# Tying five chunks' router logits to the shared expert's progress, and adding three chunks' shared results later, in a fused spike and mixture-of-experts kernel

## The chip, the cores and the metric

The kernel runs on one core of a Trainium2 chip. The core has five engines that this document names often: TensorE (PE in the profile; its weight loads are shown apart as PEld), VectorE (DVE), ScalarE (ACT), GpSimd (POOL) and SyncE (SP), whose queue issues most transfers. The metric is the device time of one launch in microseconds; less is better.

## The reference, cut to what matters

The input `x` is 16 sequences of 256 rows with 256 columns in f32, together 4096 rows. A first layer adds spikes to it, and a second adds a mixture of experts with one shared expert:

```python
rates = relu(x) * 0.001
c = cond[:, None, :] + cumsum(rates, axis=1)
spikes = floor(c) - previous_floor(c)          # along the 256 rows
x = x + spikes / 0.001

shared = silu(xf @ w1) * (xf @ w3) @ w2        # 256 -> 512 -> 256
s = sigmoid(concat([xf, cond], -1) @ router_W) # 8 experts
_, topk_idx = top_k(s + router_bias, 2)
gates = s_sel / (sum(s_sel) + 1e-9)
h = gelu(xf @ W1e[e]);  y = h @ W2e[e]         # the two experts of a row, 256 -> 256 -> 256
x = x + (shared + gates[0] * y[0] + gates[1] * y[1]) / 3
```

## The kernel before, in words

The 4096 rows are cut into 8 chunks of 512 (`NCHUNK`, `N`). A chunk i passes these steps.

- `Spikes` and `elementwise(i)` (from L264 and L491). TensorE turns the chunk so that columns lie on partitions (L294), ScalarE writes rates and a copy (L301, L310), VectorE forms the running sums (L323, L332, L337), ScalarE adds the starting state and rounds (L347, L356), and VectorE takes the floor, the differences and the sum `x1` (L369, L370, L381, L389).
- `route(i)` (L522) is a generator of eight steps, taken with `next(ro)`. First the logits: 8 products of `x1` with the router's weights on TensorE (L535), then `lt` on VectorE (L544), a turn `pn` on TensorE (L547), an exponential on ScalarE (L551), some twenty small VectorE instructions that pick the two experts (L553 to L590), the places in the experts' lists on TensorE (`pr`, L596 to L602), `x1` turned back by TensorE (L618) and copied to `x1t` by ScalarE (L619), the rows' addresses `at_i` on VectorE (L632), and eight indirect stores of `x1t` into the buffer `xs` in DRAM, issued by POOL (L636), some 1.28 us apart.
- The shared expert, `shared_hidden(i)` and `shared_out(i)`. A hidden step is, for each of four column blocks u, two pairs of products (L659, into `ph`), a silu on ScalarE (L669) and a multiplication on VectorE (L670, into `hs`). An output step is 16 products (L686, into `pa`, two halves of 512 columns), and for each half a VectorE instruction that multiplies by a third and adds to `x1t` (L697). All products are f32, and a product is two instructions in the profile.

The shared expert has no deadline until the end, and the kernel uses it to fill TensorE. `all_shared()` (L717) yields its steps in the order hidden 0, hidden 1, out 0, hidden 2, out 1 and so on, and `unit(n)` (L728) takes n units from it wherever the program calls it. One unit is 4 hidden products or 8 output products. With `whole` left true, a unit that ends a pair also emits the ScalarE and VectorE instructions behind it.

The program has five stages. A head (L744 to L806) handles chunk 0 and begins chunk 1. A loop (L829) runs route(i-1), elementwise(i) and (i+1) and units. In the tail (from L853) the last chunk's route runs, then the experts' counts (`pcnt`, L866), a table of 128-row blocks on VectorE (L873 to L917), two small products (L920, L924), and between these the units `unit(0.5)` (L858), `unit(2, whole=False)` (L862), `unit(2.5)` (L918) and `unit(3)` (L927). Then come the expert blocks (`run_blocks`): six blocks are loaded ahead by transfers on SP's queue and on ScalarE's (L956), `unit(1)` fills TensorE once more, and then for each block VectorE copies the weights (L971, `load_w`) and turns the rows (L976), TensorE multiplies (L1003, `up`), ScalarE applies gelu (L1011), TensorE multiplies (L1025, `down`), ScalarE copies (L1033) and POOL stores the result (L1034). A last stage gathers the results, combines them with the gates (L1141) and runs what is left of the shared expert.

In the head and in the tail with the blocks, the order on TensorE, ScalarE and VectorE is the order of the program (`manual_schedule`). In the loop a planner decides when the program is built: each engine takes, of what is ready by the planner's own clock, what stands earliest in the program. It may take instructions of the loop into gaps of the head. At run time every engine executes its list in order and waits on semaphores.

Outputs leave when both the shared and the routed part of a row tile are done (`part_done`, L707), which is in the last stage for all chunks.

Of the kernel before, what the change touches and what calls it, by code (L numbers as in the profile page):

```python
# [38 lines left out]
def kernel(  # L39
# [83 lines left out]

    busy = const.tile([P, N], BF16)
    nc.vector.memset(busy, 0.0)
# [136 lines left out]
    class Spikes:  # L262
# [256 lines left out]

    placed = {}  # L520

    def route(i):  # L522
        x1, x1t = x1s[i], x1ts[i]

        def small(tag, shape=(P, J, E), dt=F32):
            return rt.tile(list(shape), dt, tag=tag, name=f"{tag}_{i}")

# [5 lines left out]
        for k in range(KD):  # L533
            for j in range(J):
                nc.tensor.matmul(  # L535
                    pl[ts(j, 32), :],
                    lhsT=rw[:, k, :],
                    rhs=x1[:, k, ts(j, P)],
                    start=(k == 0),
                    stop=(k == KD - 1),  # L540
                )
        yield
        lt = small("lt", (P, P))
# [99 lines left out]

    hts = {}

    def shared_hidden(i, slices):
# [3 lines left out]
        for cols in slices:  # L652
            n = cols.stop - cols.start
            for u in range(KS):
                ps = []
                for w in (w1_sb, w3_sb):
                    ph = p_h.tile([P, n], F32, tag="ph", name=f"ph_{i}_{u}_{cols.start}_{len(ps)}")
                    for k in range(KD):
                        nc.tensor.matmul(  # L659
                            ph,  # L660
                            lhsT=w[:, k, ts(u, P)],
                            rhs=x1[:, k, cols],
                            start=(k == 0),
                            stop=(k == KD - 1),
                        )
                    ps.append(ph)
                    yield n / N / 2, len(ps) == 2
# [9 lines left out]
    def shared_out(i):  # L677
# [4 lines left out]
        for h in range(J // n):  # L682
            pa = p_acc.tile([P, n, D], F32, tag="acc", name=f"pa_{i}_{h}")
            for q in range(n):
                for s in range(KS):
                    nc.tensor.matmul(  # L686
                        pa[:, q, :],
# [13 lines left out]
            yield 0, False  # L701


# [125 lines left out]
    for i in range(2, NCHUNK):  # L829
# [14 lines left out]
        next(nxt, None)  # L844
        unit(1 + (i > 3 and i % 3 != 2) + (i == NCHUNK - 1))
        next(ro)
# [64 lines left out]

    diag = const.tile([P, P], BF16)
# [3 lines left out]
    rows_f = const.tile([P, NBLK], F32)  # L916
# [9 lines left out]
    nc.vector.tensor_copy(rows_i[:, :NBLK], prow)  # L926
    unit(3)  # L927

# [271 lines left out]
```

## Time and profile before

| what | us |
|---|---|
| median of 10 runs | 332.92 (332.72 to 333.17) |
| the profiled execution | 332.96 |
| its span in the profile | 331.2 |
| busy: PE, PEld, DVE, ACT, POOL | 322.8, 236.9, 224.5, 142.4, 160.4 |
| last logits (L535) start | 129.54 |
| first expert block (L1003) starts | 163.37 |
| last stage's products (L659) start | 283.07 |

The span is the time from the first to the last instruction. A line of the timeline gives start, duration, engine, source line, operation, output and inputs, how many instructions were merged, and in brackets how long the engine was idle ahead and what ended that. "PEld ... issue" is time in which nothing that the profile shows was waited for. An engine name with a q is its queue issuing transfers. The granted TensorE clock was full in every slice.

### The profile page before, as it was taken

To read this page: it belongs to the slowest core of one execution; us is meant where nothing else is said; L and a number is where in the kernel's file an instruction comes from. 1 tells how busy PE (TensorE), PEld (TensorE's weight loads), DVE (VectorE), ACT (ScalarE), POOL (GpSimd) and SP (SyncE) were. 2 spreads that over 40 slices of the span, in tenths; PEclk is the share of its full clock that TensorE was granted. 3 is DMA by queue.
4 is the path that set the end of the run, shared out by engine and by line. 5 is a ranking of instruction groups with operands and counts; after the bars stand their busy time and mean duration, and the time that the engine had idled before them with its cause. 6 is when DMAs were issued, how large, how long until landed. Compare 5 with 4: busy or idle time off the path is not lost. (4 is left out here: it accounts for less than half of the span.)

```text
span 331.2 us, 6640 instructions
## 1 busy us (share of the span) xinstructions
PE 322.8 (97%) x1734; PEld 236.9 (72%) x1734; DVE 224.5 (68%) x612; ACT 142.4 (43%) x301; POOL 160.4 (48%) x199
## 2 busy tenths in 40 slices
PE   8999999999999999999999999999999999999996
PEld 3877554546646645746699999999999999465485
DVE  5786879889999994642467654554555552089993
ACT  4449294948568363040244444444444444301100
POOL 6000671787877777172045555555555555223220
PEclk9999999999999999999999999999999999999999
DMA  7561827474212122054446667766666752499933
GB/s 235 165 145 48 225 100 189 152 213 154 95 54 98 66 83 102 30 194 108 75 101 146 149 156 161 149 153 129 153 148 144 169 144 83 135 376 410 405 113 127
DMA packets 62550, 50.36 MB, mean 152 GB/s; under 512 B 42622, under 2 KB 52879, under 8 KB 62512
## 3 DMA queue, kind: packets, MB, share of 16 engines
q1 hardware_dynamic: 42928, 26.21, 31.6%
q0 software_dynamic: 7456, 20.86, 17.2%
q10 hardware_dynamic: 12128, 2.86, 5.1%
q8 instruction: 15, 0.25, 0.3%
q14 instruction: 23, 0.19, 0.2%
HBM read 27.44 MB, written 22.84 MB: 152 GB/s over the span
## 5 line engine op out<-in xcount | busy, mean ns | idle before, releaser
L659 PE MATMUL ph<-x,w_sb 128*128 128x512 f32 (+2 forms) x320 | 118.8, 513 | 1.6 <-DVE x L487 0.7
L1034 POOL DMA_INDIRECT ys<-yb,to x67 | 65.9, 984 | 67.1 <-ACT yb L1033 57.3
L636 POOL DMA_INDIRECT xs<-x1t,at_i x64 | 74.3, 1162 | 42.0 <-issue 16.8
L659 PEld LDWEIGHTS ph<-x,w_sb 128*128 128x128 f32 x320 | 53.6, 190 | 44.0 <-issue 38.1
L1003 PEld LDWEIGHTS phe<-xbt,w1e 128*128 128x128 f32 x536 | 70.3, 191 | 4.7 <-ACT hbt L1011 0.9
L1003 PE MATMUL phe<-xbt,w1e 128*128 128x128 f32 x536 | 70.7, 275 | 0.7 <-DVE xbt L976 0.7
L1025 PE MATMUL py<-we,hbt 128*128 x268 | 68.8, 380 | 0.0
L686 PE MATMUL pa<-w_sb,hs 128*128 128x256 f32 x256 | 59.7, 383 | 0.0
L971 DVE COPY w1e<-we 128x512 f32 x67 | 28.8, 431 | 44.8 <-PE phe L1003 44.3
L686 PEld LDWEIGHTS pa<-w_sb,hs 128*128 128x128 f32 x256 | 47.4, 190 | 9.5 <-issue 3.8
L669 ACT ACTIVATE as<-ph 128x512 f32<-128x512 f32 (+2 forms) x40 | 20.5, 516 | 68.1 <-PE ph L659 65.0
L1025 PEld LDWEIGHTS py<-we,hbt 128*128 128x128 f32 x268 | 45.9, 191 | 3.6
L1011 ACT ACTIVATE hbt<-phe 128x256 f32<-128x256 f32 x67 | 25.7, 383 | 44.7 <-PE phe L1003 36.3
L670 DVE TENSOR_TENSOR hs<-as,ph 128x512 f32<-128x512 f32 (+2 forms) x40 | 23.0, 575 | 29.8 <-PE ph L659 23.4
L1033 ACT COPY yb<-py 128x256 f32<-128x256 f32 x67 | 24.9, 372 | 23.1 <-PE py L1025 23.0
L976 DVE STREAM_TRANSPOSE xbt<-xb 128x256 f32<-128x256 f32 x67 | 29.3, 437 | 0.2
L323 DVE TENSOR_TENSOR_SCAN tb<-keep,rates 128x1024 f32<-128x1024 f32 (+1 forms) x9 | 17.3, 1925 | 0.0
L712 POOL DMA_DIRECT2D out_dram<-yc x8 | 5.8, 727 | 22.7 <-DVE yc L1141 22.7
L573 POOL COPY x1t<-first 128x16 f32<-128x16 f32 x8 | 4.4, 548 | 24.5 <-DVE first L571 24.5
L347 ACT ACTIVATE tb<-tb,cond_t 128x256 f32<-128x256 f32 x30 | 13.1, 498 | 6.4 <-DVE tb L337 6.4
L697 DVE SCALAR_TENSOR_TENSOR x1t<-pa,x1t 128x512 f32<-128x512 f32 x14 | 9.6, 684 | 7.7 <-PE pa L686 7.7
L619 ACT COPY x1t<-px 128x512 f32<-128x512 f32 x16 | 8.9, 585 | 7.7 <-PE px L618 7.7
(152 smaller groups left out, 278.7 us busy)
## 6 DMA issues: line engine op xcount, KB each, us to landing
xb<-xs SPq DMA_DIRECT2D x184, 33.0 KB
yc<-ys SPq DMA_DIRECT2D x8, 512.0 KB
we<-ys SPq DMA_DIRECT2D x8, 512.0 KB
xn<-in_x_dram SPq DMA_DIRECT2D x7, 512.0 KB
xb<-xs ACTq DMA_DIRECT2D x84, 33.0 KB
we<-in_L_cond_W1e_dram SPq DMA_DIRECT2D x8, 256.0 KB
we<-in_L_cond_W2e_dram SPq DMA_DIRECT2D x8, 256.0 KB
out_dram<-yc POOLq DMA_DIRECT2D x8, 256.0 KB, 5.5
```

The source lines that it names most:

```text
L636: nc.gpsimd.indirect_dma_start(out=xs_w[(i * J + j) * TOPK + q][:, :], out_offset=bass.IndirectOffsetOnAxis(ap=at_i[:, q, j : j + 1], axis=0),
L659: nc.tensor.matmul(ph, lhsT=w[:, k, ts(u, P)], rhs=x1[:, k, cols], start=(k == 0), stop=(k == KD - 1),)
L669: nc.scalar.activation(act, ps[0], AF.Silu)
L670: nc.vector.tensor_tensor(ht[:, u, cols], act, ps[1], ALU.mult)
L686: nc.tensor.matmul(pa[:, q, :], lhsT=ht[:, s, ts(n * h + q, P)], rhs=w2_sb[:, s, :], start=(s == 0), stop=(s == KS - 1),)
L971: nc.vector.tensor_copy(w, we[:, bass.ds(off, KD * HE)])
L976: nc.vector.transpose(xt.rearrange("p g k r -> p g (k r)"), block[b].pop("xb")[:, :, :FQ])
L1003: nc.tensor.matmul(ph[:, m, :].rearrange("p (g r) -> p g r", r=Q), lhsT=w[:, k, ts(m, P)], rhs=xt[:, :, k, :], start=(k == 0), stop=(k == ...
L1011: nc.scalar.activation(ht, ph, AF.Gelu)
L1025: nc.tensor.matmul(py, lhsT=ht[:, k, :], rhs=we[:, bass.ds(off + KD * HE + k * D, D)], start=(k == 0), stop=(k == KH - 1),)
L1033: nc.scalar.copy(yb, py)
L1034: nc.gpsimd.indirect_dma_start(out=ys_w[b][:, :], out_offset=bass.IndirectOffsetOnAxis(ap=to[:, b : b + 1], axis=0), in_=yb, in_offset=Non ...
```

## The change

A counter `made` collects the shared expert's products in program order. `STEP` names, for chunks 2 to 6, a number of products; the logits of that chunk get an ordering edge (no wait at run time) that lets the planner place them on TensorE only after that product. In the loop, each i from 3 on takes half a unit more; the tail takes 1.5 units in place of 2.5, and three half units in place of 3. The results of chunks 0, 1 and 2 (`LATER`) are no longer added to `x1t` by VectorE out of the accumulator: ScalarE writes them, times a third, over the chunk's `x1`, which nobody reads any more, and VectorE adds them (`add_third`) in the tail, two after each half unit. So that `x1` stays that long it has 8 buffers in place of 6, `first` and `at_i` have 8 in place of 2, and three small tiles move into buffers of other tiles. The condition that held back chunk 0's addition until chunk 1 was placed is gone.

```diff
-    busy = const.tile([P, N], BF16)
+    busy = hid.tile([P, N], BF16, tag="ht", name="busy")
...
-                [P, KD, N], F32, tag="x1", name=f"x1_{self.i}", bufs=6
+                [P, KD, N], F32, tag="x1", name=f"x1_{self.i}", bufs=8
...
+    logits = {i: [] for i in range(NCHUNK)}
+    STEP = {2: 84, 3: 100, 4: 120, 5: 140, 6: 156}
+    made = []
+
+    def in_step(i):
+        if i in STEP and logits[i] and len(made) >= STEP[i]:
+            for m in logits[i]:
+                tc.add_manual_dep(
+                    m.ins,
+                    made[STEP[i] - 1].ins.name,
+                    mybir.DependencyInfo(
+                        mybir.DependencyClass.NoSync, mybir.DependencyReason.DATA
+                    ),
+                    reason="order on TensorE",
+                )
+
+    def shared_matmul(*args, **kwargs):
+        made.append(nc.tensor.matmul(*args, **kwargs))
+        for i, n in STEP.items():
+            if n == len(made):
+                in_step(i)
...
-        key_first = small("first", (P, J))
+        key_first = small("first", (P, J), bufs=NCHUNK)
...
-        at_i = small("at_i", (P, TOPK, J), I32)
+        at_i = small("at_i", (P, TOPK, J), I32, bufs=NCHUNK)
...
+    LATER = 3
+    thirds = []
...
-            with tc.issue_after(placed[1].ins) if i == 0 else nullcontext():
-                nc.vector.scalar_tensor_tensor(
-                    bs, pa.rearrange("p q (g f) -> p q g f", f=FQ), THIRD, bs, ALU.mult, ALU.add
-                )
+            if i < LATER:
+
+                third = x1s[i].rearrange("p k n -> p (k n)")[:, ts(h, n * D)]
+                nc.scalar.activation(third, pa.rearrange("p q d -> p (q d)"), AF.Copy, scale=THIRD)
+                thirds.append((i, h * n, bs, third))
+                yield 0, False
+                continue
+            nc.vector.scalar_tensor_tensor(
+                bs, pa.rearrange("p q (g f) -> p q g f", f=FQ), THIRD, bs, ALU.mult, ALU.add
+            )
             part_done(i, h * n, n)
             yield 0, False
+
+    def add_third():
+
+        i, j, bs, third = thirds.pop(0)
+        nc.vector.tensor_tensor(
+            bs, bs, third.rearrange("p (q g f) -> p q g f", q=wide(i), f=FQ), ALU.add
+        )
+        part_done(i, j, wide(i))
...
-        unit(1 + (i > 3 and i % 3 != 2) + (i == NCHUNK - 1))
+        unit(1 + (i > 2) / 2 + (i > 3 and i % 3 != 2) + (i == NCHUNK - 1))
...
-    unit(2.5)
+    unit(1.5)
...
-    unit(3)
+    for _ in range(LATER):
+        unit(0.5)
+        add_third()
+        add_third()
```

In `shared_hidden` and `shared_out` the products are made by `shared_matmul`, and the logits of `route` are kept in the list `logits[i]`, followed by a call of `in_step(i)`. The tiles `diag` and `rows_f` of the tail take buffers of the tile `lt`.

More of the change, by code (lines that the diff above doesn't have):

```diff
@@ L1 @@
 import itertools
-from contextlib import ExitStack, nullcontext
+from contextlib import ExitStack
 import numpy as np
@@ L520, with small @@
     placed = {}
+    logits = {i: [] for i in range(NCHUNK)}
[17 more added lines that the diff above has]
+                in_step(i)
     def route(i):
         x1, x1t = x1s[i], x1ts[i]
-        def small(tag, shape=(P, J, E), dt=F32):
-            return rt.tile(list(shape), dt, tag=tag, name=f"{tag}_{i}")
+        def small(tag, shape=(P, J, E), dt=F32, **kw):
+            return rt.tile(list(shape), dt, tag=tag, name=f"{tag}_{i}", **kw)
         def wide(a):
@@ L534, in route @@
             for j in range(J):
[L535 to L540, printed above, removed]
+                logits[i].append(
+                    nc.tensor.matmul(
+                        pl[ts(j, 32), :],
+                        lhsT=rw[:, k, :],
+                        rhs=x1[:, k, ts(j, P)],
+                        start=(k == 0),
+                        stop=(k == KD - 1),
+                    )
                 )
+        in_step(i)
         yield
@@ L658, in shared_hidden @@
                     for k in range(KD):
-                        nc.tensor.matmul(
+                        shared_matmul(
                             ph,
@@ L685, in shared_out @@
                 for s in range(KS):
-                    nc.tensor.matmul(
+                    shared_matmul(
                         pa[:, q, :],
@@ L694, in shared_out @@
             bs = final.get((i, h * n), x1ts[i][:, ts(h, n), :, :FQ])
[L696 to L699 removed]
+            if i < LATER:
[7 more added lines that the diff above has]
+            )
             part_done(i, h * n, n)
             yield 0, False
+    def add_third():
+        i, j, bs, third = thirds.pop(0)
+        nc.vector.tensor_tensor(
+            bs, bs, third.rearrange("p (q g f) -> p q g f", q=wide(i), f=FQ), ALU.add
+        )
+        part_done(i, j, wide(i))
     done = {t: 0 for t in range(NTT)}
@@ L910 @@
     nc.vector.tensor_copy(table, table_f)
-    diag = const.tile([P, P], BF16)
+    diag = rt.tile([P, P], BF16, tag="lt", name="diag")
     nc.vector.tensor_scalar(which, which, -1.0, float(E), ALU.mult, ALU.add)
     nc.vector.tensor_scalar(diag, ident, which, None, ALU.mult)
-    rows_f = const.tile([P, NBLK], F32)
+    rows_f = rt.tile([P, NBLK], F32, tag="lt", name="rows_f")
     nc.vector.tensor_scalar(rows_f, ident[:, :NBLK], table_f[:, 0:1], None, ALU.mult)
-    unit(2.5)
+    unit(1.5)
     pcode = p_t.tile([P, NBLK], F32, tag="pt", name="pcode")
```

## The prediction

> **What bounds the kernel now.** I read the page's busy shares first, then the busy time by stretch, then TensorE's waits and its instructions in order of time, and last the other engines around the hand-over to the expert blocks.
>
> ```profile
> PE 322.8 (97%) x1734; PEld 236.9 (72%) x1734; DVE 224.5 (68%) x612; ACT 142.4 (43%) x301; POOL 160.4 (48%) x199
> ...
> 36.40:129.50 93.10, 91.66 (x427) 50.16 (x426) 83.02 (x190) 58.89 (x102) 66.40 (x59) 1.00 0.42 127
> 129.50:163.40 33.90, 33.90 (x142) 21.75 (x142) 13.81 (x51) 6.05 (x11) 10.91 (x12) 1.00 0.37 103
> 163.40:282.10 118.70, 117.96 (x805) 110.71 (x803) 66.44 (x216) 51.20 (x134) 63.97 (x65) 1.00 0.62 141
> ...
> PE pr L597 <- DVE hot L590: 1.1, 3, 0.6
> PE pn L547 <- DVE lt L544: 0.2, 1, 0.2
> ```
>
> After the clock interval each window line gives busy time of PE, PEld, DVE, ACT and POOL. TensorE is busy all the time, but its ends are modelled, so I look at the distance between starts. In the combine stage, where the chain that ended last is TensorE alone, 24 hidden instructions take from 283.07 to 293.47, 0.43 us each, and 32 output ones 0.216 us. In the middle stretch the same spacings hold: 22 hidden instructions between 119.92 and 129.54 are again 0.43 apart. Subtracting such spacings from the starts between 36.4 and 129.5 leaves only 2.7 us in which TensorE stood for another engine (0.72 at 53.2, 0.39, 0.53 and 0.25 ahead of L597, 0.37 ahead of L547, some 0.4 in smaller ones; the two wait lines are the part that outlasts the modelled ends). VectorE is 89% busy there, but TensorE reaches the last chunk's logits 3.6 us after their input was ready: the last L389 ends at 125.94, L535 starts at 129.54.
>
> The next two fences are the hand-over in order of time: TensorE, then POOL, SP's queue, VectorE and ScalarE.
>
> ```profile
> 119.92 9.69 PE L659 MATMUL ph<-x,w_sb 128*128 128x512 f32 x22
> 129.54 0.64 PE L535 MATMUL pl<-x,rw 128*32 128x128 f32 x16
> 130.12 1.99 PE L686 MATMUL pa<-w_sb,hs 128*128 128x256 f32 x8
> 131.95 0.27 PE L547 MATMUL pn<-ident,lt 128*128 128x128 f32 x1
> ...
> 139.05 0.40 PE L596 MATMUL pr<-region,ones_r 1*128 1x32 f32 x2
> ...
> 140.43 0.17 PE L866 MATMUL pcnt<-counts_b,ones_b 128*128 128x8 bf16 x1
> ...
> 159.94 3.60 PE L659 MATMUL ph<-x,w_sb 128*128 128x512 f32 x8
> 163.37 1.05 PE L1003 MATMUL phe<-xbt,w1e 128*128 128x128 f32 x8
> 165.16 1.13 PE L1003 MATMUL phe<-xbt,w1e 128*128 128x128 f32 x8 [0.74 <-DVE xbt L976]
> 166.22 1.10 PE L1025 MATMUL py<-we,hbt 128*128 x4
> ```
>
> ```profile
> 150.49 0.97 POOL L636 DMA_INDIRECT xs<-x1t,at_i  x1 [0.30 <-issue]
> ...
> 152.94 15.76 SPq L956 DMA_DIRECT2D xb<-xs  x26
> ...
> 163.64 0.69 DVE L670 TENSOR_TENSOR hs<-as,ph 128x512 f32<-128x512 f32 x1 [1.63 <-PE ph L659]
> ...
> 153.09 5.51 ACTq L956 DMA_DIRECT2D xb<-xs  x7
> 161.85 0.60 ACT L669 ACTIVATE as<-ph 128x512 f32<-128x512 f32 x1 [9.74 <-PE ph L659]
> ...
> 163.22 1.28 ACT L1011 ACT_TABLE_LOAD   x1 [0.77 <-issue]
> 164.51 0.38 ACT L1011 ACTIVATE hbt<-phe 128x256 f32<-128x256 f32 x1
> ```
>
> This is a second path beside TensorE: logits, route, eight scatters on POOL, their landing, the block loads. The loads start at 152.94, the moment the last scatter has landed; by the landing marks in the trace block 0 is complete at 156.4, block 1 at 158.4, block 3 at 161.5. TensorE comes to block 0 only at 163.37, since the written order puts 6.5 units of the shared expert (1 unit is 8 hidden or 16 output instructions, 3.44 us either way) between pcnt and it. So the path of the data has some slack, and the change spends it.
>
> **The change part by part.** The sum is made against the profiled execution, 332.96 us (span 331.2 and 1.76 around it); the median of the runs is 332.92, no difference.
>
> *Units moved.* The loop gets half a unit more in each of i = 3 to 7; the tail gives back one at the 2.5 and one and a half at the 3. Adding up the units, 160 products stand before the last logits now (a product is two instructions) and 178 then: 16 output products of chunk 3, 32 x 0.216 = 6.91, and 2 hidden ones of chunk 5, 4 x 0.43 = 1.72. TensorE's total is unchanged, but the last logits, and with them the whole second path, come 8.63 us later, less what the middle can absorb. Behind them wait lt, the route on VectorE, POOL's eight scatters, SP's and ScalarE's block loads.
>
> *What the middle absorbs.* The ties put logits of chunks 2 to 6 behind 84, 100, 120, 140 and 156 products; counted in the timeline they stand behind 76, 90, 107, 122 and 140. TensorE then has more to do between two routes and VectorE less, so the 2.7 us of waits can shrink; a whole x1 also keeps the logits in one piece, where now three of five are cut in two (0.92 against 0.57 to 0.75 us), up to 0.7. Bounds 0 and 3.4 us; I take the middle, 1.7, because L597's waits are a chain (lt, exp, twenty small ones) that the ties don't shorten.
>
> *Three chunks' results on ScalarE.* Six L697 leave VectorE's middle, 6 x 0.68; six scaled copies of 128x512 out of PSUM come to ScalarE, bounded by L619 (0.585) and L669 (0.60): 3.6 us on an engine busy 58.9 of 93.1. Nothing in the middle waits for them but the two accumulation buffers, which chunk 0 holds until 56 now. Without that cover the price were 3.6. Since TensorE is the later engine, VectorE's saving is worth nothing by itself; what it could bring is inside the 1.7. No DMA moves: these chunks' outputs leave only in the combine stage.
>
> *Six adds in the tail*, L381 as the nearest row (0.683): 4.1 us on a VectorE busy 13.81 of 33.9, done before block 0 lands. Two or three fall beside the last scatters. Those take 0.97 to 1.50 beside L381 and L389, 0.97 alone: 0 to 0.5, I take 0.2.
>
> *lt behind a product.* Now the unit after the last logits is an output product; lt runs at 130.32 beside it and pn follows at 131.95, 2.41 after the logits began. Then it is the second half of a hidden pair: logits 0.58, four instructions 1.72, 0.18 to the start of L670, 0.6 until lt can start, 0.34, 0.05: pn at 3.47. That adds 1.06 on the second path (0.6 to 1.2 by how early L670 starts). If the planner leaves that pair whole, it is 0.
>
> *The cover at the blocks.* After pcnt TensorE has 4 units instead of 6.5: 14.3 us with the two small products, so on the old clock it stands before block 0 at 154.8, where the data is complete at 156.4. Then the order written out bites: ScalarE issues seven block loads until 158.6 before it may take the hidden activation (L669), VectorE's L670 waits for that (159.3), and load_w(1) and block 1's turn stand behind L670. Today L670 starts at 163.64 and block 1 at 165.16; so block 1 at 160.8. ScalarE's next two loads reuse marks that land at 160.6, then a table load of 1.28 and gelu 0.38: down(0) at about 162.7, today 166.22. The second path gains 3.5 us against TensorE's order, not 8.63. Bounds: 4.3, if gelu is in time, and 3.2, if the loads land 0.3 later. From there the distance of the blocks is 1.75 us as now, all else hidden under TensorE.
>
> *The rest* (the tiles busy, diag and rows_f in other buffers, x1, first and at_i with more) costs no instruction. VectorE's waits in the middle are for ScalarE and TensorE only, never for these buffers, so nothing is gained. POOL: chunk 6's scatters end some 22 us after its logits, chunk 7's begin about 27 after them.
>
> Sum: 8.63 - 1.7 + 0.2 + 1.06 - 3.5 = +4.7, 337.6 us. Its ends: 8.63 - 3.4 + 0 + 0.6 - 4.3 = +1.5 (334.5), and 8.63 - 0 + 0.5 + 1.2 - 3.2 = +7.1 (340.1).
>
> [...]
>
> **The rivals.** *The last logits overtake* (other side): the planner may run them when x1 is ready, ahead of free products. The place is TensorE's order at product 178; each output product overtaken takes 0.43 us off the second path. From 11 on it wins; if all 18 are overtaken the path starts as now, less the 1.7: 331.3 us. For it: their input is ready early. Against: now too they waited 3.6 us for 160 of 160.
>
> *The cover is not needed.* If ScalarE's loads don't hold up L669 and the blocks start as soon as TensorE is there, only the 1.7 and today's wait of 0.9 go: 330.4. Against: block 0 lands 1.6 us after TensorE is ready.
>
> *ScalarE becomes late*: its copies stand before exp or a silu, buffers come free late, some 0.5 us per route for six routes on top of the sum: 340.6. For it: VectorE already waits 0.6 to 1.6 us for L551. Against: 63% load.
>
> *It doesn't do what it says*: the planner finds no place for 18 more products before the last logits and leaves them behind, so neither the path nor the cover moves: 333. Against: its buffers come free earlier than now.
>
> **How the numbers follow.** The sum's case 0.65; milder forms of it, without the lt wait or with pairs overtaken, 333.6 to 334.5, 0.10; overtaking 0.08; cover not needed 0.06; no change 0.05; ScalarE late 0.06. Less than 0.2%, 0.7 us, can't be told from no change. Faster 0.14, same 0.05, slower 0.81. The likeliest case alone spans 334.5 to 340.1; the range with a fair part of the others is 332.6 to 340.2.
>
> **What would show it.** Right: the last L535 about 6 to 8 us later, at 135.5 to 138; L547 stalled about 1 us behind lt; a gap on TensorE before the first L1003 and a second before block 1 with VectorE's xbt as releaser, some 5 us together; L1025 starting near 170.5; the blocks and the combine stage as long as now. Wrong: L535 with fewer than 178 products before it, no gap at the blocks, or waits in the middle that were larger than the 2.7 us I count.

## The result and the profile after

The changed kernel takes 345.66 us (median of 8 runs, 344.60 to 346.37) against 333.04 us of the kernel before (28 runs, 332.72 to 333.77) on the same chips: a ratio of 1.0376, interval 1.0367 to 1.0386. It is 12.6 us slower; the forecast was 4.7 us slower, with 340.2 as its upper end. The profiled execution took 345.54 us (span 343.8), 12.58 above that of before.

The page's busy times and granted clock come first.

```profile
PE 324.6 (94%) x1734; PEld 238.9 (69%) x1734; DVE 225.5 (66%) x612; ACT 146.2 (43%) x307; POOL 159.2 (46%) x199
...
PEclk9999999999999999999959999999999999999999
```

TensorE's busy time has hardly moved (322.8 before), so the loss is idle time; and one slice of the clock reads 5, which no slice of before did. Next the busy time by stretch (after each clock interval PE, PEld, DVE, ACT, POOL, then the clock), cut at the last logits, at block 0, shortly before the return of the clock, and ahead of the combine stage; and TensorE's waits up to the last logits.

```profile
36.40:139.90 103.50, 99.23 (x466) 56.85 (x466) 82.31 (x187) 61.41 (x106) 63.09 (x58) 1.00 0.38 112
139.90:169.10 29.20, 25.55 (x106) 14.59 (x105) 15.52 (x54) 6.13 (x9) 13.03 (x14) 1.00 0.34 110
169.10:180.00 10.90, 6.37 (x27) 5.55 (x28) 4.16 (x13) 2.91 (x5) 0.41 (x1) 0.57 0.44 75
180.00:295.00 115.00, 114.96 (x779) 107.73 (x778) 62.36 (x203) 49.06 (x130) 63.81 (x66) 1.00 0.63 143
```

```profile
PE pr L623 <- DVE hot L616: 2.6, 4, 0.8
PE pn L573 <- DVE lt L570: 1.2, 2, 1.0
```

Line numbers have shifted: L559 is the logits, L573 `pn`, L570 `lt`, L616 `hot`, L623 `pr`, L540 every product of the shared expert, L697 its silu, L698 its multiplication, L739 the late adds, L1000 the block loads, L1020 a block's turn, L1047 and L1069 its two pairs of products, L1055 its gelu. Before the last logits TensorE waits more than before (1.1 and 0.2 us on these two lines then). Behind them it has 3.65 idle us where it had none, then 4.53 in the eleven around the first blocks. The next fence is the hand-over to the blocks, first on TensorE, then on POOL, ScalarE with its queue (ACTq) and VectorE.

```profile
139.88 0.65 PE L559 MATMUL pl<-x,rw 128*32 128x128 f32 x16
...
143.64 0.30 PE L573 MATMUL pn<-ident,lt 128*128 128x128 f32 x1 [1.21 <-DVE lt L570]
...
152.13 0.17 PE L907 MATMUL pcnt<-counts_b,ones_b 128*128 128x8 bf16 x1
...
163.05 3.60 PE L540 MATMUL ph<-x,w_sb 128*128 128x512 f32 x8
169.09 1.16 PE L1047 MATMUL phe<-xbt,w1e 128*128 128x128 f32 x8 [2.45 <-DVE xbt L1020]
174.46 2.04 PE L1047 MATMUL phe<-xbt,w1e 128*128 128x128 f32 x8 [4.21 <-DVE xbt L1020]
176.83 2.07 PE L1069 MATMUL py<-we,hbt 128*128 x4 [0.33 <-ACT hbt L1055]
...
162.24 1.50 POOL L662 DMA_INDIRECT xs<-x1t,at_i  x1 [0.30 <-issue]
...
165.22 6.98 ACTq L1000 DMA_DIRECT2D xb<-xs  x7
172.30 0.60 ACT L697 ACTIVATE as<-ph 128x512 f32<-128x512 f32 x1 [17.55 <-DMA xb<-xs]
172.82 2.25 ACTq L1000 DMA_DIRECT2D xb<-xs  x2
175.10 1.28 ACT L1055 ACT_TABLE_LOAD   x1 [2.19 <-DMA xb<-xs]
...
176.39 0.66 ACT L1055 ACTIVATE hbt<-phe 128x256 f32<-128x256 f32 x2
...
168.59 0.45 DVE L1020 STREAM_TRANSPOSE xbt<-xb 128x256 f32<-128x256 f32 x1 [3.11 <-DMA xb<-xs]
172.93 0.69 DVE L698 TENSOR_TENSOR hs<-as,ph 128x512 f32<-128x512 f32 x1 [3.90 <-ACT as L697]
...
173.88 0.44 DVE L1020 STREAM_TRANSPOSE xbt<-xb 128x256 f32<-128x256 f32 x1
```

It is the picture forecast, only larger: a gap before each of the first two blocks with the turn as releaser, ScalarE's seven load issues ahead of the silu, the silu ahead of VectorE's multiplication, that ahead of block 1's turn. One thing is new: block 1's products last 2.04 us here, where a block's products last 1.05 before. The clock was at half. Two stretches of one us show when (columns as above):

```profile
170.00:171.00 1.00, 0.25 (x3) 0.06 (x1) 0.00 (x0) 0.00 (x0) 0.00 (x0) 0.82 0.43 79
...
180.00:181.00 1.00, 1.00 (x5) 0.91 (x5) 0.35 (x2) 0.35 (x1) 0.59 (x1) 0.56 0.62 95
```

The stretch before the first reads 1.00 and those between the two 0.50, so the clock fell at about 170.65 and came back at about 180.9. At 170.65 the second gap had lasted only 0.4 us: the fall came behind the first gap of 2.45 us and the beginning of the second, with 3.8 of the second's 4.21 us still ahead.

Following the path event by event gives the account. The columns are start times in two profiled executions, and the third is what the step between adds.

| event | before | after | step adds |
|---|---|---|---|
| last logits | 129.54 | 139.88 | +10.34 |
| `pn` of that chunk | 131.95 | 143.64 | +1.35 |
| `pcnt` | 140.43 | 152.13 | +0.01 |
| first block load | 152.94 | 165.22 | +0.58 |
| block 0's second products | 166.22 | 176.83 | -1.67 |
| block 10's first products | 181.21 | 193.81 | +1.99 |
| combine stage | 283.07 | 295.67 | 0.00 |

They add up to 12.60. The 10.34 holds the 8.63 us of moved products, so the middle did not absorb but lost 1.71.

### The profile page after: what moved, and what is told of

The parts are those of the page before. It is cut to its first block, busy times and chain, and to the rows that moved or that the text cites. A ratio compares the mean times of both kernels' runs of the same rounds, so it can differ in the third digit from the quotient of the medians.

```text
span 343.8 us, 6630 instructions
## 1 busy us (share of the span) xinstructions
PE 324.6 (94%) x1734; PEld 238.9 (69%) x1734; DVE 225.5 (66%) x612; ACT 146.2 (43%) x307; POOL 159.2 (46%) x199
## 5 line engine op out<-in xcount | busy, mean ns | idle before, releaser
L540 PE MATMUL ph<-x,w_sb 128*128 128x512 f32 (+2 forms) x320 | 118.7, 513 | 2.5 <-DVE x L487 1.2
L662 POOL DMA_INDIRECT xs<-x1t,at_i x64 | 72.0, 1125 | 53.5 <-issue 16.1
L540 PEld LDWEIGHTS ph<-x,w_sb 128*128 128x128 f32 x320 | 53.9, 190 | 46.6 <-issue 38.8
L1047 PEld LDWEIGHTS phe<-xbt,w1e 128*128 128x128 f32 x536 | 71.9, 196 | 11.1 <-issue 4.4
L1047 PE MATMUL phe<-xbt,w1e 128*128 128x128 f32 x536 | 72.6, 280 | 6.7 <-DVE xbt L1020 6.7
L1069 PE MATMUL py<-we,hbt 128*128 x268 | 70.1, 385 | 0.3 <-ACT hbt L1055 0.3
L540 PE MATMUL pa<-w_sb,hs 128*128 128x256 f32 x256 | 59.4, 382 | 0.0
L540 PEld LDWEIGHTS pa<-w_sb,hs 128*128 128x128 f32 x256 | 47.5, 190 | 9.0 <-issue 3.2
L1069 PEld LDWEIGHTS py<-we,hbt 128*128 128x128 f32 x268 | 46.6, 194 | 4.3 <-ACT hbt L1055 0.6
L697 ACT ACTIVATE as<-ph 128x512 f32<-128x512 f32 (+2 forms) x40 | 20.6, 514 | 66.9 <-PE ph L540 49.1
L1055 ACT ACTIVATE hbt<-phe 128x256 f32<-128x256 f32 x67 | 25.6, 384 | 44.0 <-PE phe L1047 34.7
L698 DVE TENSOR_TENSOR hs<-as,ph 128x512 f32<-128x512 f32 (+2 forms) x40 | 23.0, 577 | 31.1 <-PE ph L540 20.3
L1020 DVE STREAM_TRANSPOSE xbt<-xb 128x256 f32<-128x256 f32 x67 | 29.3, 437 | 3.6 <-DMA xb<-xs 3.6
L599 POOL COPY x1t<-first 128x16 f32<-128x16 f32 x8 | 5.5, 690 | 26.4 <-DVE first L597 26.4
L369 DVE TENSOR_TENSOR tb<-tc,tb 128x1024 f32<-128x1024 int32 (+1 forms) x8 | 9.3, 1156 | 6.4 <-ACT tc L356 6.4
```

What stands on the lines that cost most here:

```text
L540: made.append(nc.tensor.matmul(*args, **kwargs))
L662: nc.gpsimd.indirect_dma_start(out=xs_w[(i * J + j) * TOPK + q][:, :], out_offset=bass.IndirectOffsetOnAxis(ap=at_i[:, q, j : j + 1], axis=0),
L697: nc.scalar.activation(act, ps[0], AF.Silu)
L698: nc.vector.tensor_tensor(ht[:, u, cols], act, ps[1], ALU.mult)
L1020: nc.vector.transpose(xt.rearrange("p g k r -> p g (k r)"), block[b].pop("xb")[:, :, :FQ])
L1047: nc.tensor.matmul(ph[:, m, :].rearrange("p (g r) -> p g r", r=Q), lhsT=w[:, k, ts(m, P)], rhs=xt[:, :, k, :], start=(k == 0), stop=(k == ...
```

## The experiments

Times are medians, ratios are to the kernel before in the same comparison. A diff is against the kernel that the text names. The values ahead of a block, or between two events, are from the profiled execution of that run.

**The parts alone.** Only the moved units, on the kernel before:

```diff
-        unit(1 + (i > 3 and i % 3 != 2) + (i == NCHUNK - 1))
+        unit(1 + (i > 2) / 2 + (i > 3 and i % 3 != 2) + (i == NCHUNK - 1))
...
-    unit(2.5)
+    unit(1.5)
...
-    unit(3)
+    unit(1.5)
```

> The kernel before with the moved units alone (half a unit more from i = 3 on, 1.5 and 1.5 in the tail); no ties, no results put aside. If moving the units makes the loss: last logits at 137 to 139 (129.54 before), two gaps on TensorE at the first blocks of 5 us or more together, the granted clock falling there, 341 to 345 us. If the ties and the ScalarE copies make it: last logits near 136, 337 us or less.

341.58 us, 1.026 (1.0243 to 1.0277): +8.7. TensorE in the trace of this run:

```profile
137.30 0.64 PE L535 MATMUL pl<-x,rw 128*32 128x128 f32 x16
...
165.96 1.16 PE L1003 MATMUL phe<-xbt,w1e 128*128 128x128 f32 x8 [1.90 <-DVE xbt L976]
171.08 2.05 PE L1003 MATMUL phe<-xbt,w1e 128*128 128x128 f32 x8 [3.96 <-DVE xbt L976]
173.56 1.70 PE L1025 MATMUL py<-we,hbt 128*128 x4 [0.43 <-ACT hbt L1011]
```

The last logits come 7.76 later, so without ties the middle absorbs 0.87 of the 8.63. The `pn` step costs the same 1.35 here, and from the first loads (162.04) to block 0's second products it is 11.52 us, where before it was 13.28: 1.76 hidden, against the 3.5 forecast. The units alone make most of the loss.

Without the ties, on the kernel after:

```diff
-    STEP = {2: 84, 3: 100, 4: 120, 5: 140, 6: 156}
+    STEP = {}
```

> The changed kernel with an empty STEP, all else kept. If the ties cause the longer middle (last logits at 139.88, 1.7 us beyond the 8.63 that the units cost), the last logits come at 136.5 to 138.5 and the time is 342 to 344. If the middle is long for another reason (the planner sets the next chunk's sum ahead of the last instruction of a route), it stays at 345 to 346.

343.49 us, 1.0321 (1.0303 to 1.0339). The last logits are at 137.29 as with the units alone, so the copies do nothing to the middle. The ties are worth 2.2 us of the time (345.66 less 343.49), and they show in the middle: last logits 2.59 later. Against the units alone this run loses 1.9: the first block load 0.58 later (the same 13.09 after `pcnt` as in the kernel after, where it was 12.51 before), and 17.02 instead of 15.59 us from block 0's second products to block 10, with the half clock lasting 10.24 us (6.83 with the units alone).

The ties alone on the kernel before, and the kernel after with the units put back:

```diff
+    STEP = {2: 84, 3: 100, 4: 120, 5: 140, 6: 156}
...
+        in_step(i)
...
-                        nc.tensor.matmul(
+                        shared_matmul(
```

> The kernel before with the ties alone, same five numbers. If the ties make TensorE wait for hot in the middle: last logits 1 to 2.5 us later, 333.5 to 335.5. If they only fill it better, as the change hopes: 332.9 or less.

```diff
-        unit(1 + (i > 2) / 2 + (i > 3 and i % 3 != 2) + (i == NCHUNK - 1))
+        unit(1 + (i > 3 and i % 3 != 2) + (i == NCHUNK - 1))
...
-    unit(1.5)
+    unit(2.5)
...
-        unit(0.5)
+        unit(1)
```

> The changed kernel with the units as in the kernel before (2.5 in the tail, then three whole units with the additions behind each); ties and copies kept. If moving the units makes the loss: no gap of more than 1 us at the blocks, full clock, 332 to 336. If ties and copies make a good part of it: 338 or more, with the last logits well behind 129.5.

335.38 us (1.0076, 1.0059 to 1.0092) and 334.56 us (1.0046, 1.003 to 1.0063). Waits of TensorE up to the last logits, taken roughly from distances of starts as in the prediction, are about 5 us in both and in the kernel after, against some 2.4 before and 1.7 to 2 in the two runs without ties. So wherever the ties are, TensorE waits longer, and the forecast that they would shorten the waits is refuted. Not all of it arrives at the last logits: these come 0.84 and 1.31 us later than before (130.38 and 130.85) with the old units, and 2.59 later with the moved ones. In both runs POOL is still busy with chunk 6's stores when chunk 7's could start, and the loads come 5 us later than before (158.31 and 157.72), but the full cover hides nearly all of that: block 0's second products come 1.57 and 1.55 us later, about as much as `pcnt` (1.47 and 1.53).

The late adds and ScalarE's copies alone (kernel after, no ties, units back):

```diff
-    STEP = {2: 84, 3: 100, 4: 120, 5: 140, 6: 156}
+    STEP = {}
...
-        unit(1 + (i > 2) / 2 + (i > 3 and i % 3 != 2) + (i == NCHUNK - 1))
+        unit(1 + (i > 3 and i % 3 != 2) + (i == NCHUNK - 1))
...
-    unit(1.5)
+    unit(2.5)
...
-        unit(0.5)
+        unit(1)
```

> The changed kernel with the units as before and without ties: ScalarE's copies and the late additions alone. If VectorE's shorter middle is worth something: last logits 0.3 to 1 us earlier and 332 to 332.7. If the copies only move work between engines that nobody waits for: 332.8 to 333.2. If the additions beside the scatters cost on the path of the data: 333.5 or more.

333.06 us, 1.0003 (0.9995 to 1.0012): nothing, and the last logits are at 129.63. This closes the rival in which ScalarE's copies make it late.

**Why the ties cost waits.** VectorE in the kernel after, chunk 2's route (start, duration, line):

```profile
67.29 0.19 DVE L614 SCALAR_TENSOR_TENSOR chosen<-run,key 128x32 f32<-128x32 f32 x1
67.40 2.28 DVE L323 TENSOR_TENSOR_SCAN tb<-keep,rates 128x1024 f32<-128x1024 f32 x1
69.60 0.17 DVE L616 TENSOR_TENSOR hot<-chosen 128x32 bf16<-128x32 f32 x1
```

A later chunk's running sum, 2.28 us, is ordered one instruction ahead of `hot`, and TensorE waits 0.95 us for `hot` before it goes on at 69.82. The scan stands in this place in the routes of chunks 3 and 4 too (82.58 and 100.31; waits of 0.62 and 0.85). The kernel before has no scan right ahead of these three (for chunk 2 its `hot` runs at 64.32 and the scan at 66.68). The longest wait of the kernel after is another, 1.17 us ahead of 126.70 for `lt`, which stands behind a 1.23 us L369 and a 0.68 us L698. To see whether this order is the cause, the scan and the floors were held behind `hot` of earlier chunks by ordering edges on VectorE, in the kernel before:

```diff
-        sp.scan(part)
+        with behind_hot(i - 2):
+            sp.scan(part)
...
-        sp.floor(part)
+        with behind_hot(i - 1):
+            sp.floor(part)
```

> The kernel before with two ordering edges on VectorE: floor of chunk i behind hot of chunk i-1, and the sum of chunk i behind hot of chunk i-2. If TensorE's waits ahead of L597 in the middle come from those long instructions being taken first: they shrink from 1.9 us to under 0.7, last logits 1 us or more earlier, 331 to 332.3. If VectorE's order does not matter or its later x1 is worse: 333 or more.

333.34 us, 1.0013 (1.0004 to 1.0023). The waits for `hot` fall to about 0.2 us each, and the profile's list of waits, where they were 1.1 us before, names them no more; so the order is the cause of those waits. The time does not fall: VectorE's sums for a later chunk come later instead (TensorE now waits 0.5 us for `x` of L389), and the last logits stay 0.3 us behind. That the same edges would take the waits out of the kernel after was not tried, so for the ties this cause is read from the trace and not shown by a run.

**The cover at the blocks.** One unit moved ahead of the last logits, on the kernel before:

```diff
-        unit(1 + (i > 3 and i % 3 != 2) + (i == NCHUNK - 1))
+        unit(1 + (i > 3 and i % 3 != 2) + 2 * (i == NCHUNK - 1))
...
-    unit(3)
+    unit(2)
```

> The kernel before with one unit moved from the last 3 of the tail into the last pass of the loop. By the account of the path (last logits to first L1069 has some 1.7 us of room in the kernel before: 13.28 us from first block load to L1069 there, 11.6 where TensorE waits for the data): last logits 3.45 later, of which 1.7 is hidden, no half clock, 334.3 to 335.3. If the room is over 3.5 us: 332.9 to 333.2.

336.53 us, 1.0102 (1.0087 to 1.0117), above the 335.3 expected. The loads start 3.42 us later, at 156.36, block 0's second products at 167.86: 11.50 apart, as with all units moved. So 1.78 of the 3.42 us are hidden, as much as with all units moved (1.76). Here is what follows them, TensorE's timeline and one stretch of the busy times with its clock:

```profile
165.39 1.13 PE L1003 MATMUL phe<-xbt,w1e 128*128 128x128 f32 x8 [0.99 <-DVE xbt L976]
167.86 2.08 PE L1025 MATMUL py<-we,hbt 128*128 x4 [1.34 <-ACT hbt L1011]
169.72 1.76 PE L1003 MATMUL phe<-xbt,w1e 128*128 128x128 f32 x8
```

```profile
168.00:171.30 3.30, 3.30 (x12) 2.94 (x13) 0.09 (x1) 0.45 (x2) 0.68 (x1) 0.52 0.33 58
```

Behind two waits of 0.99 and 1.34 us, with 1.13 us of work between, the clock reads 0.52 over 3.3 us, and block 10 is 1.64 us later against block 0's second products than before.

What sets the 11.5? It is no fixed need of the path. In the two runs with ties and the old units the same stretch takes 9.48 and 10.05 us (158.31 to 167.79, 157.72 to 167.77). ScalarE's seven load issues take 5.19 and 5.33 us there, 6.77 with one unit or all units moved, 6.98 in the kernel after. The traces of the kernels before and after show what the issues wait for. In both, the 268 loads of the blocks share eight semaphores (the prediction's marks), 33 or 34 loads each, on which their landings are recorded; and three of ScalarE's first nine issues in the kernel after start 0.02 us after the earlier load on the same semaphore has landed. There the seventh issue comes 6.65 us after the first load, behind a load of SP that was issued at 4.64 and landed at 6.63; the ninth comes at 9.52, behind one that landed at 9.50. In the kernel before, counted in the same way, the seventh shares its semaphore with a load issued at 2.81 and landed at 4.79, and comes at 5.33. The loads are the same in both; which of them share a semaphore is not. This is read from the traces, and no run varied it alone.

Edits of the order tell more. First the unit of the block stage was written ahead of the block loads, in the kernel after, then with four blocks loaded ahead instead of six:

```diff
+        if first == 0:
+            unit(1)
         for b in range(first, min(first + AHEAD, end)):
             load_block(b, first, end)
...
-            if b == 0:
-                unit(1)
```

> The changed kernel with the one unit of the block stage written ahead of the block loads, so that its silu and its L698 stand before ScalarE's seven loads. If the second gap is block 1 waiting behind that L698 alone: block 1 at 171 instead of 174.46 and 342 or less. If the first gelu is held by ScalarE's nine block loads as well: block 1 earlier, but the first L1069 still at 176 to 177 and 344.5 to 346.

```diff
-    AHEAD = 6
+    AHEAD = 4
```

> As the run before, and four blocks loaded ahead in place of six, so that six of ScalarE's loads stand before the first gelu, not nine. If these loads hold the gelu: first L1069 2 us or more earlier than in the run before, no or a shorter half clock, 341.5 to 343.5. If the blocks' landing is what holds TensorE: no earlier, 345 or more.

343.65 us (1.0329, 1.0312 to 1.0347) and 345.79 us (1.0386, 1.0329 to 1.0443). The first lies between its two expectations; the second misses its theory's 341.5 to 343.5. With the first, ScalarE and TensorE read:

```profile
164.96 0.60 ACT L697 ACTIVATE as<-ph 128x512 f32<-128x512 f32 x1 [10.21 <-PE ph L540]
166.26 6.55 ACTq L1000 DMA_DIRECT2D xb<-xs  x9
172.84 1.28 ACT L1055 ACT_TABLE_LOAD   x1 [7.28 <-DMA xb<-xs]
...
171.35 2.05 PE L1047 MATMUL phe<-xbt,w1e 128*128 128x128 f32 x8 [0.94 <-DVE xbt L1020]
174.57 2.07 PE L1069 MATMUL py<-we,hbt 128*128 x4 [1.17 <-ACT hbt L1055]
```

Block 1 starts 3.1 us earlier than in the kernel after, as soon as its rows are turned. The second products gain only 2.26, because now gelu, behind nine load issues and the table load, ends last. With four blocks ahead they come at 173.19, but the later blocks starve (106.2 us from block 10 to the combine stage, where the kernel after has 101.9). The same move in the kernel before, and in the kernel with the copies alone:

> The kernel before with the one unit of the block stage written ahead of the block loads. TensorE's wait of 0.9 us ahead of block 1 came from L670 standing before load_w(1). If that is so: no wait there, 332.0 to 332.3, faster than before. If another wait takes its place: 332.9 or more.

> The two runs before joined: copies and late additions, units as before, no ties, and the block stage's unit ahead of the loads. If both gains are real and add up: 331.2 to 332. If the copies bring nothing: as the run with the unit first alone.

340.87 us (1.0249, 1.0222 to 1.0275) and 341.62 us (1.0255, 1.0231 to 1.0279): the gain expected did not come, and the loss is some 8 us. ScalarE in the former:

```profile
161.84 0.60 ACT L669 ACTIVATE as<-ph 128x512 f32<-128x512 f32 x1 [9.74 <-PE ph L659]
163.42 6.55 ACTq L956 DMA_DIRECT2D xb<-xs  x9
170.01 1.28 ACT L1011 ACT_TABLE_LOAD   x1 [7.57 <-DVE xbt L976]
```

There the cover is long, so a silu written ahead of ScalarE's loads holds them until TensorE has made its input at 161.8, though the rows were ready at 153. The order on ScalarE's queue is right with one length of cover and wrong with another.

Then the silu and the multiplication alone were moved, behind block 1's turn, with the products left in place; in the kernel before, and the same lines in the kernel after:

```diff
             if b == 0:
-                unit(1)
+                unit(1, whole=False)
             if b + 1 < end:
                 load_w(b + 1)
+            if b == 1:
+                unit(0)
```

> The kernel before with one move: the silu and the multiplication that end the hidden unit of the block stage are written after block 1's weight copies and turn instead of ahead of them (the products stay where they are). In the kernel before TensorE waits 0.74 us ahead of block 1 for VectorE's turn of block 1, which stands behind the 0.69 us multiplication L670. Theory (the wait is VectorE's order): block 1 starts 0.7 to 0.9 us earlier against block 0, block 10 too, and the time is 332.0 to 332.4. Rival (the wait passes on to the gelu of block 0 or to block 1's second products, since ScalarE's table load of 1.28 us comes next): 332.9 to 333.4. A worse rival: the silu behind the gelu's table load costs a second table load of 1.3 us on ScalarE, and a later gelu waits: 333.5 to 335.

> The kernel after with the same move of the activation and the multiplication behind block 1's turn. Theory (two queues hold the hand-over: VectorE's turn of block 1 stands behind the multiplication, and gelu stands behind ScalarE's seven load issues, the activation, two more issues and the table load): block 1 starts as soon as its data is there, at about 170 to 171 in place of 174.5, but block 0's second products still wait for gelu until 176 to 176.8, so of the 4.2 us gap only some tenths come back: 344.7 to 345.7. Rival (the turn alone held the blocks): second products at about 173, 341.5 to 343.

The kernel before with it takes 331.82 us (7 runs, 331.65 to 332.57), 0.9963 (0.995 to 0.9976): 0.4% faster than the kernel before, a small gain but clear of the noise. TensorE and VectorE:

```profile
163.33 1.95 PE L1003 MATMUL phe<-xbt,w1e 128*128 128x128 f32 x16
165.12 1.03 PE L1025 MATMUL py<-we,hbt 128*128 x4
...
163.60 0.69 DVE L670 TENSOR_TENSOR hs<-as,ph 128x512 f32<-128x512 f32 x1 [0.56 <-PE ph L659]
```

Blocks 0 and 1 run without a gap (x16 is both), and the second products start 1.10 us earlier. So the 0.74 us wait in front of block 1 was VectorE's order. (In the profiled execution, the slowest of the seven, some of it is lost again later, 0.5 us in one wait for gelu.) The kernel after, on the other hand, goes to 346.50 us (1.0404, 1.0387 to 1.0421), and both theories missed it:

```profile
165.65 9.87 ACTq L1000 DMA_DIRECT2D xb<-xs  x9
175.63 0.60 ACT L697 ACTIVATE as<-ph 128x512 f32<-128x512 f32 x1 [20.45 <-DMA xb<-xs]
...
176.28 2.08 PE L1047 MATMUL phe<-xbt,w1e 128*128 128x128 f32 x8 [5.41 <-ACT as L697]
```

The silu, written later, now has nine load issues ahead of it instead of seven. VectorE turned block 1 at 171.00, but TensorE began it only at 176.28, when the silu had ended (176.23; the multiplication had only just begun, at 176.26). That block 1 needs the accumulator which the silu reads is how I understand it, not shown by a run of its own. With a short cover, then, it is ScalarE's list that holds the blocks. Two more runs take load issues off it, first those of the first six blocks, then all:

```diff
-            (nc.sync if q < NQ - 1 - (b % AT == AT // 2) else nc.scalar).dma_start(
+            (nc.sync if b < AHEAD or q < NQ - 1 - (b % AT == AT // 2) else nc.scalar).dma_start(
```

> The kernel after with all loads of the first six blocks on SP's queue (24 there in place of 17, none on ScalarE's); later blocks as before. Theory (the cover ends where ScalarE's load issues end): the hidden activation runs at about 167 in place of 172.3, the multiplication ends by 168, block 1 starts when its data lands (about 171.5, four issues of 0.6 a block), gelu is not late, and block 0's second products start at 172 to 173 in place of 176.8; the gaps of TensorE ahead of blocks 0 and 1 are 2 to 3 us each and the blocks then follow their loads every 2.3 us or so until block 6. Time 341.5 to 344.0. Rival (the loads' landing holds the blocks, not ScalarE's order): second products no earlier than 175.5, time 344.5 to 346.5, since SP's queue is then the slower one.

```diff
-            (nc.sync if q < NQ - 1 - (b % AT == AT // 2) else nc.scalar).dma_start(
+            nc.sync.dma_start(
```

> The kernel after with every load of the expert blocks on SP's queue, none on ScalarE's. With only the first six blocks' loads moved, the activation ran at 165.31, block 1 started at 172.10, but the gelu of block 0 stood behind ScalarE's two loads of blocks 6 and 7, which waited until 177.52, and the second products came at 180.13. Theory (what stands ahead of gelu on ScalarE's queue holds the blocks): with no load there gelu of block 0 runs by 172, its second products start at 172.2 to 173.2 in place of 176.8, and from there the blocks follow SP's loads, some 2.0 to 2.3 us each, until the store of loads catches up; time 341 to 344.5 by how long they stay behind. Rival (the landing of the loads holds block 0's second products too): they start after 175.5 and the time is 345 or more.

348.29 us, 1.0456 (1.0439 to 1.0474), a miss: silu, multiplication and block 1 (172.10) come early as expected, but ScalarE's two loads of blocks 6 and 7 still stand ahead of gelu and now issue only at 177.52, and the second products come at 180.13. With all loads on SP 400.26 us, 1.1807 (1.1721 to 1.1893); in that comparison the kernel before took 340.36 us too, and in the trace the last logits come at 148.03, 8.15 us later than in the kernel after and long before any block load, for a reason that is not known. So only distances within this trace are used. SP's queue, ScalarE and TensorE:

```profile
175.10 14.89 SPq L1000 DMA_DIRECT2D xb<-xs  x25
...
175.41 1.28 ACT L1055 ACT_TABLE_LOAD   x1
181.62 0.38 ACT L1055 ACTIVATE hbt<-phe 128x256 f32<-128x256 f32 x1 [4.92 <-PE phe L1047]
...
183.75 1.91 PE L1069 MATMUL py<-we,hbt 128*128 x4
```

The table load is done long before gelu's input, and the second products follow the first load by 8.65 us instead of 11.61. So 2.96 of the 11.61 go with ScalarE's load issues. The time expected was missed by over 55 us all the same: with one queue a block takes 2.52 us (143.36 us from block 10 to the combine stage, 57 blocks) where with two it takes 1.79. VectorE's turns wait for loads 44 times between 190 and 348 us there, 63.1 us in all; how much of that is owed to whatever slowed this comparison is open.

**The half clock.** Products that nobody reads were put into TensorE's gaps of the kernel after; nothing is left out. First two before block 0 and four before block 1, then three and five, and two more before block 0's second products:

```diff
+    def fill(n):
+        idle = p_acc.tile([P, N], F32, tag="acc", name=f"fill_{n}")
+        for _ in range(n):
+            nc.tensor.matmul(idle, lhsT=ident, rhs=keep[:, :N], start=True, stop=True)
...
+            if b == 1 or b == 2:
+                fill(2 * b)
```

> The changed kernel with products of constants that nobody reads put into the two gaps of TensorE, 2 (1.7 us) ahead of block 0 and 4 (3.4 us) ahead of block 1. If the half clock from 170.8 to 180.4 comes from these gaps and costs time: full clock throughout and 341.5 to 343. If the clock falls for another reason or costs nothing: 345 to 346, half clock still there.

```diff
+            if b == 1 or b == 2:
+                fill(1 + 2 * b)
...
+            if b == 2:
+                fill(2)
```

> The kernel after with products that nobody reads put into TensorE's gaps at the hand-over (3 of 128x512 before block 0, 5 before block 1, 2 before block 0's second products); nothing else changes, and the work they add is more than the gaps hold only by some tenths of a us. Theory (half clock costs 2.0 us of the 12.6): the granted clock is full in every slice, block 10 starts 15.0 us after block 0's second products as in the kernel before (17.0 in the kernel after), and the time is 343.3 to 343.9. Rival (the slow blocks at the start are starved by their loads, and the clock is hidden beside that): full clock, but the distance stays at 16.5 to 17 us and the time at 345.2 to 345.8. If the fills outlast the gaps, the second products of block 0 start later than 176.8 and the time shows it one for one.

The small fill takes 343.75 us (1.0317, 1.03 to 1.0334), above the 343 expected and unevenly: four executions with a mean clock of 0.999 or more took 343.42 to 343.78, two with 0.995 took 345.40 and 346.45. The larger fill takes 343.79 us (1.0319, 1.0303 to 1.0335), 343.70 to 343.91 in all five, at a full clock. TensorE in it:

```profile
170.16 4.46 PE L1117 MATMUL fill<-keep,ident 128*128 128x512 f32 x10
174.46 1.05 PE L1047 MATMUL phe<-xbt,w1e 128*128 128x128 f32 x8
175.35 1.88 PE L1117 MATMUL fill<-keep,ident 128*128 128x512 f32 x4
177.07 1.03 PE L1069 MATMUL py<-we,hbt 128*128 x4
```

Block 1 starts when it did, at 174.46, the second products even 0.24 us later, and yet block 10 comes at 191.98 instead of 193.81: 14.91 us, as in the kernel before (14.99). The half clock costs 1.9 us of the 12.6 (345.66 less 343.79), and the blocks are not starved behind it.

## Why the prediction was wrong

The direction and the path that carries the loss were right, at 0.81 for slower; the size was not, and the range ended 5.5 us too low. Two steps had the mechanism wrong: what the ties do in the middle, and the clock behind the gaps, which stood at nothing. The prediction's own sign of being wrong, waits in the middle above 2.7 us, came true with about 5. Step by step:

- **Units moved, +8.63.** Right. The units alone give +7.76 at the last logits, 8.63 less an absorption of 0.87.
- **What the middle absorbs, -1.7 (0 to -3.4).** Wrong, and the largest miss: +1.71, so 3.4 us. Without ties it was -0.87, inside the bounds. The argument for the ties ("TensorE then has more to do between two routes and VectorE less") looked at amounts of work; what changed, as the trace shows it, was VectorE's order, in which a later chunk's 2.28 us scan fell ahead of `hot` in three routes. I named a chain that the ties don't shorten but gave it no price above zero: the bound should have reached to a loss of about the 2.6 us that the ties cost at the last logits, and one scan per route was a row to take it from.
- **Adds beside the scatters, +0.2 (0 to 0.5).** 0.58, just beyond the bound: the last scatter took 1.50 us, the duration that the prediction named, and the loads came 13.09 instead of 12.51 us after `pcnt`. The rival that makes ScalarE late is refuted by the copies alone (1.0003).
- **`lt` behind a product, +1.06 (0.6 to 1.2).** The mechanism is exact, TensorE 1.21 us behind `lt`, with L698 at 142.55 just ahead of it. The step is 1.35, 0.15 beyond the bound, and the same in the run with the units alone.
- **Cover at the blocks, -3.5 (-4.3 to -3.2).** Wrong by 1.8: it was -1.67, -1.76 with the units alone and -1.78 with a single unit moved. The order was traced rightly: loads, silu, multiplication, turn. The sizes of two terms failed. ScalarE's seven issues were taken at 5.5 us, as in the kernel before; they took 6.98, the seventh behind a landing at 6.63. The two that follow ended at 175.07, 9.85 us after the first load, where the prediction had them released at 7.7. These two stand ahead of gelu. With the ties alone, where the seven took 5.19 us, the stretch was 9.48, and the prediction's 3.5 off the old 13.28 makes 9.8.
- **"From there the distance of the blocks is 1.75 us as now".** Wrong: +1.99, the half clock. I forecast two gaps of 5 us in all and did not ask what they would do to the clock; the fill shows that the half clock costs 1.9 us.

The traces show after what idle time the clock halved, and that it came back under work. In the kernel after it fell 0.4 us into the second gap, with one whole gap of 2.45 us behind it, and came back 6.4 us after block 1's products had begun. Without the ties it fell at 168.09, when a single gap of 2.90 us and block 0's products lay behind it and the second gap was about to begin. With one unit moved no gap was longer than 1.34 us, and the clock still read 0.52 from 168.0 to 171.3. From which length on a gap brings the clock down, no run shows.

Of the rivals, overtaking and a change without effect are out by the last logits at 139.88 with every moved product ahead of them, and no need of the cover by the two gaps at the blocks. Together, 3.4 of the middle, 1.8 of the cover, 2.0 of the clock, 0.4 of the adds and 0.3 of `lt` are the 7.9 us between the forecast and the measured 12.6.

## What to carry to other kernels

Work that fills an engine ahead of a hand-over is cover for a second path: before moving it, follow that path's queues instruction by instruction, load issues included, and expect only the slack that is left after the last of them (1.8 us here, of 8.6 moved). A gap on TensorE can cost more than its length: here 10.24 us of half clock came with the two gaps, and 1.9 us of the time with it, so price both. An edge that holds one engine's instruction back changes the lists of the others: look at what the planner puts into the place, not only at how much work there is.

## What the runs showed of the hardware

- The clock fell 0.4 us into TensorE's second wait after a first of 2.45 us (the kernel after), 0.8 us into the second after a first of 1.90 (units alone), after a single wait of 2.90 us (no ties), and after 0.99 and 1.34 us within 3.5 us (one unit moved). With the small fill's remaining waits of 0.87, 1.03 and 1.24 us it fell in two executions of six, by their mean clock. The half clock lasted 10.24, 6.83, 10.24, 3.41 and, in the small fill's profile, 3.41 us, which is 3, 2, 3, 1 and 1 times 3.41. Where the clock read 0.50, a block's products lasted 1.91 to 2.07 us in the kernel after; at full clock 1.03 to 1.16.
- No activation ran from the first to the last of ScalarE's load issues at the hand-over: seven in 5.51 us in the kernel before, seven in 6.98 in the kernel after, nine in 9.87 with the silu moved there. Three issues of the kernel after start 0.02 us after the earlier load on the same semaphore has landed (4.49 after 4.47, 6.65 after 6.63 and 9.52 after 9.50, counted from the first load).
- The last indirect store of chunk 7 took 1.50 us to issue on POOL, from 162.24 on, next to VectorE's 128x512 adds (L739 until 162.90, L730 from 163.25); the one before it took 1.02 beside four such adds, and 0.97 is the median of the kernel before. Whether the adds slow the one store, and what in them, is open.
